# Attention projections: queries and keys computed for whole heads side by side and brought to their partitions by transfers

## The chip, the cores and the metric

The kernel runs on one core of one Trainium2 chip. The metric is the device time of one execution in microseconds (us); the time before is the median of three runs.

## What is computed

Four sequences of 512 tokens with 288 channels go through a transformer layer whose normalizations are shifted and scaled by a condition vector, and then through a rotation. Cut to what matters here:

```python
mod = silu(c) @ w_adaln + b_adaln                      # six vectors of 288 for each sequence
h = modulate(ln(x), sh_msa, sc_msa)
q, k, v = heads(h @ w_qkv + b_qkv)                     # 16 heads of 18 channels
o = softmax(q @ k.T * 18 ** -0.5) @ v
x = x + g_msa * (o @ w_proj + b_proj)
xn = modulate(ln(x), sh_mlp, sc_mlp)
x = x + g_mlp * top2_of_4_experts(xn)                  # hidden width 1152, gelu
U, _ = qr(P)                                           # P is 288 x 64
R = expm(skew(silu(c) @ W.T + b))                      # 64 x 64 for each sequence
x = x + ((x @ U) @ R - x @ U) @ U.T
```

## The kernel before, in words

Everything is float32, and the order of work on every engine is the order in which the program is written (`manual_schedule`): each engine and each DMA-issuing queue runs its own instructions in that order, and waits for others by semaphores.

**Attention.** A sequence (batch b, 0 to 3) is handled in four groups g of four heads, and a group in four key tiles t of 128 tokens: n = 4b + g, 64 steps (n, t) in all. A head has 18 channels but stands in a quarter of 32 partitions, so that a group fills the 128 partitions and four heads' small products run in the four quarters of TensorE at once. In each step `weigh` (line 1670) makes the scores z of four heads (line 1678, two tiles of two heads), ScalarE takes their exponentials es (line 1687), and `gather` (line 1691) adds the products with the values of the step before into av (line 1696). z has two buffers, so the scores of a step wait for the exponentials of the one before.

**Projections.** `project` (line 1645) makes a group's queries and keys: two products of three matmuls (line 1655), each 96 rows (a third of the 288 channels) by 128 columns (four heads of 32, 14 of each 32 columns being zeros in the padded weight `wqk`) by 512 tokens. ScalarE writes them to the tile `qk` and adds the bias (line 1662). So a batch takes eight such products. `begin` (line 1611) normalizes the next batch, turns it (`modulate_T`, line 1140, transposes into hT) and makes the values, with an add of the bias by VectorE (line 1632). The weights come zero-padded from the host.

**What else runs beside.** The lists `steps` and `beside` in the loop (lines 2172 to 2220) say, step by step, which pieces follow the scores: `steps[g, t]` holds those bound to a batch, `beside` gives one piece per step in order, after those of `steps`. They are:

- `divide` (`normalize`, line 1704): the softmax's sums. ScalarE copies av to oraw in the first step of the next group, SP moves the four rows of sums to den by four transfers (line 1718), VectorE inverts them two steps later (line 1724), SP moves them back to rr (line 1728), and VectorE spreads rr and multiplies in the step after (lines 1735 and 1736).
- `column` (line 1480): one reflection of the QR factorization, some 25 dependent VectorE instructions; the first such piece only scales pT.
- `merge`, `residual`, `route` (lines 1748, 1740, 1766): output projection po, the second normalization, the choice of experts. Its last pieces leave `where`, the slots of half of the tokens, and POOL then scatters rows to DRAM one by one (line 2008), which `load_slots` fetches again as xg.
- In `beside`: `other_modulation` (line 1189; products pr with `wadb`, then modrows, then POOL's DMAs through DRAM, lines 1213 and 1214), `skew_matrices` (line 1218; the load wr, the product pa in step 2.2 of batch 0, then 66 small stores udr by SP, line 1266, in eight pieces in the next eight steps, then the load um), and the matrix exponential (`rotations`, pieces pf, pw, ph, psq), which goes back and forth between TensorE and VectorE.

**The start.** SP loads the condition, the first part of the modulation's weights, the first batch, the first group's part of `wqk` (line 985), the rest of it (991), `wadb` (993), the biases badr (997), pT (1002), the other batches (1004) and small ones. VectorE clears the first values' tile vt (line 1045), POOL the second, and POOL's constants follow. `shift_scale`, the transposes, `project(0)` and the values precede the first step.

**After the attention** come the experts, in eight blocks, with TensorE busy throughout, the rest of the QR's columns beside them on VectorE, and at the end the rotation.

Of the kernel before, what the change touches and what calls it, by code (L numbers as in the profile page):

```python
# [10 lines left out]
F32 = mybir.dt.float32  # L11
# [7 lines left out]
P = 128  # L19
HD = 18  # L20
# [793 lines left out]
def fast_path(  # L814
# [139 lines left out]
    with ExitStack() as s1:  # L954
# [17 lines left out]
        bqk = const.tile([P, 2, NG], F32, name="bqk")  # L972
        nc.scalar.dma_start(out=bqk, in_=b_qk)
# [8 lines left out]
        wqk = wat.tile([CC, NK, 2, NG * P], F32, name="wqk")  # L982
        wqv = w_qk.rearrange("(k p) t f -> p k t f", p=CC)
        for i in range(2):
            nc.sync.dma_start(out=wqk[:, :, i, :P], in_=wqv[:, :, i, :P])
        wv = wat.tile([CC, NK, C], F32, name="wv")
        nc.scalar.dma_start(out=wv, in_=w_v.rearrange("(k p) f -> p k f", p=CC))
        bv = const.tile([P, C], F32, name="bv")
        nc.scalar.dma_start(out=bv, in_=b_v.partition_broadcast(P))
        for i in range(2):  # L990
            nc.sync.dma_start(out=wqk[:, :, i, P:], in_=wqv[:, :, i, P:])
        wadb = ada.tile([CC, NK, 4 * C], F32, name="wadb")
        nc.sync.dma_start(out=wadb, in_=wad[:, :, 2 * C :])
        badr = ada.tile([P, C], F32, name="badr")
        nc.gpsimd.memset(badr, 0.0)
        for i in range(4):
            nc.sync.dma_start(
                out=badr[i * HQ : i * HQ + B, :],
                in_=b_adaln[ds((2 + i) * C, C)].partition_broadcast(B),
            )  # L1000
        pt = rot.tile([D, C], F32, name="pt")
        nc.sync.dma_start(out=pt, in_=pT)
        for b in range(1, B):
            nc.sync.dma_start(
                out=xs[:, b * NT : (b + 1) * NT, :],
                in_=x[b].rearrange("(t p) c -> p t c", p=P),
            )
        bp = const.tile([P, C], F32, name="bp")
        nc.sync.dma_start(out=bp, in_=b_proj.partition_broadcast(P))
        wgT = const.tile([CC, NK, E], F32, name="wgT")  # L1010
        nc.sync.dma_start(out=wgT, in_=w_gate)
        b1s = const.tile([P, E, NF], F32, name="b1s")
        nc.sync.dma_start(out=b1s, in_=b1T)
        nc.sync.dma_start(out=wp, in_=w_proj.rearrange("g p c -> p g c"))
# [125 lines left out]
        def modulate_T(b, which, xh, k, dst):  # L1140
            pt = bank([P, N], f"pt{which}{b}{k}")
            for t in range(NT):
                nc.tensor.transpose(
                    pt[:CC, ts(t, P)], xh[:, t, ds(k * CC, CC)], ident
                )
            nc.scalar.activation(
                dst[:, k, :],
                pt[:CC, :],
                AF.Identity,
                bias=modT[:, 2 * which, k, b : b + 1],  # L1150
                scale=modT[:, 2 * which + 1, k, b : b + 1],
            )
# [36 lines left out]
        def other_modulation():  # L1189
# [5 lines left out]
            def product():  # L1195

                pr = bank([P, N], "pr")
                for k in range(NK):
                    for i in range(4):
                        nc.tensor.matmul(  # L1200
                            pr[ts(i, HQ), :C],
                            scp[:, k, :],
                            wadb[:, k, ts(i, C)],
                            start=(k == 0),
                            stop=(k == NK - 1),
                        )
                nc.vector.tensor_add(rows, pr[:, :C], badr)
                one = rows[2 * HQ : 3 * HQ, :]
                nc.vector.tensor_scalar_add(one, one, 1.0)
# [8 lines left out]
        def skew_matrices(between):  # L1218
# [10 lines left out]
            row = skew.tile([P, width], F32, name="row")  # L1229
# [379 lines left out]
        hTs, oTs, qks, avs, xhs = {}, {}, {}, {}, {}  # L1609
        
        def begin(b):
# [3 lines left out]
            hT = a2.tile([CC, NK, N], F32, tag="hT", name=f"hT{b}", bufs=1)  # L1615
# [6 lines left out]
            def values(t):  # L1622
                pv = bank([P, C], f"pv{b}{t}")
                for k in range(NK):
                    nc.tensor.matmul(
                        pv,
                        hT[:, k, ts(t, P)],
                        wv[:, k, :],
# [3 lines left out]
                nc.vector.tensor_tensor(  # L1632
                    vt[:, t, :, 0:HD],
                    pv.rearrange("p (h d) -> p h d", d=HD),
                    bv.rearrange("p (h d) -> p h d", d=HD),
                    ALU.add,
                )
# [7 lines left out]
        def project(n):  # L1645

            b, g = divmod(n, NG)
            qk = a2.tile([P, 2, N], F32, tag="qk", name=f"qk{n}")
            qks[n] = qk

            def product(i):
                hT = hTs[b]
                pq = bank([P, N], f"pq{n}{i}")
                for k in range(NK):
                    nc.tensor.matmul(  # L1655
                        pq,
                        wqk[:, k, i, ts(g, P)],
                        hT[:, k, :],
# [3 lines left out]
                nc.scalar.activation(  # L1662
                    qk[:, i, :], pq, AF.Identity, bias=bqk[:, i, g : g + 1]
                )

            return [lambda i=i: product(i) for i in range(2)]
# [3 lines left out]
        def weigh(n, t):  # L1670


            qk, es = qks[n], []
# [362 lines left out]
        for piece in turns + project(0) + values:  # L2036
            piece()
# [134 lines left out]
        for n in range(NN):  # L2172
# [24 lines left out]
            if n + 1 < NN:  # L2197
                query, key = project(n + 1)
                steps[g, int(g == 3)].insert(0, query)
                steps[g, 2].append(key)  # L2200
# [467 lines left out]
```

## Time and profile before

| what | us |
|---|---|
| median of three runs | 731.65 (731.27 to 734.58) |
| profiled execution | 733.85 |
| its span on the core | 732.1 |
| first scores z (the loop begins) | 26.7 |
| batch 0, 1, 2, 3 begin | 26.7, 98.9, 180.6, 263.9 |
| TensorE busy of the span | 704.6 (96%) |
| VectorE, ScalarE, POOL busy | 509.2, 278.5, 216.9 |
| the projections' matmuls (line 1655), 192 | 90.7 |
| exponentials (line 1687), 128 | 124.2 |

The span is the time on the core from the first to the last instruction, and the profiled execution's own time, 1.75 us more, is the number to set it against; the median of the runs is 2.2 us below that. A group's busy time is the union of its instructions, which overlap on TensorE. The timeline of an engine merges equal instructions that follow each other: start, length, engine, line, operation, output<-inputs, shapes, count, and in brackets the engine's idle time before and what ended it. SP's rows are its issues of transfers, not the transfers.

### The profile page before, as it was taken

To read this page: it belongs to the slowest core of one execution; us is meant where nothing else is said; L and a number is where in the kernel's file an instruction comes from. 1 tells how busy PE (TensorE), PEld (TensorE's weight loads), DVE (VectorE), ACT (ScalarE), POOL (GpSimd) and SP (SyncE) were. 2 spreads that over 40 slices of the span, in tenths; PEclk is the share of its full clock that TensorE was granted. 3 is DMA by queue.
4 is the path that set the end of the run, shared out by engine and by line. 5 is a ranking of instruction groups with operands and counts; after the bars stand their busy time and mean duration, and the time that the engine had idled before them with its cause. 6 is when DMAs were issued, how large, how long until landed. Compare 5 with 4: busy or idle time off the path is not lost. (4 is left out here: it accounts for less than half of the span.)

```text
span 732.1 us, 11398 instructions
## 1 busy us (share of the span) xinstructions
PE 704.6 (96%) x3627; PEld 404.2 (55%) x3627; DVE 509.2 (70%) x2237; ACT 278.5 (38%) x427; POOL 216.9 (30%) x311
## 2 busy tenths in 40 slices
PE   6999999999999999998999999999999999999995
PEld 5432334334353444324677776777667776676763
DVE  3565678796887879685268888888888886004335
ACT  2455554454525543474222423223233232221232
POOL 4035900620026013761047064441203123031110
PEclk9999999999999999999999999999999999999998
DMA  9547700000000001144252252365324153205044
GB/s 228 149 132 196 271 3 6 1 2 2 2 1 1 3 18 60 35 147 93 61 171 70 78 179 80 131 166 165 83 77 140 28 170 78 81 29 187 37 137 146
DMA packets 65511, 66.69 MB, mean 91 GB/s; under 512 B 31625, under 2 KB 55982, under 8 KB 65441
## 3 DMA queue, kind: packets, MB, share of 16 engines
q1 hardware_dynamic: 57376, 42.48, 21.0%
q0 software_dynamic: 7360, 22.91, 9.7%
q10 hardware_dynamic: 704, 0.49, 0.3%
q8 instruction: 30, 0.49, 0.3%
q14 instruction: 41, 0.33, 0.2%
HBM read 48.08 MB, written 18.09 MB: 90 GB/s over the span
## 5 line engine op out<-in xcount | busy, mean ns | idle before, releaser
L2356 PE MATMUL pe<-w2s,hm 128*128 128x288 f32 (+1 forms) x648 | 163.7, 408 | 0.0
L1687 ACT ACTIVATE es<-z 128x1024 f32<-128x1024 f32 x128 | 124.2, 1021 | 84.6 <-PE z L1678 84.0
L2296 PE MATMUL ph<-xgT,w1s 128*128 128x288 f32 (+2 forms) x576 | 151.8, 413 | 0.4
L2356 PEld LDWEIGHTS pe<-w2s,hm 128*128 128x128 f32 (+1 forms) x648 | 118.7, 187 | 31.5 <-issue 2.3
L2296 PEld LDWEIGHTS ph<-xgT,w1s 128*128 128x128 f32 x576 | 105.8, 190 | 40.2 <-issue 11.2
L2318 ACT ACTIVATE hm<-ph,b1r 128x576 f32<-128x576 f32 (+2 forms) x72 | 49.8, 737 | 131.1 <-PE ph L2309 121.2
L1678 PE MATMUL z<-qk 32*128 32x512 f32 x512 | 90.0, 640 | 3.0 <-ACT es L1687 2.8
L1655 PE MATMUL pq<-hT,wqk 96*128 96x512 f32 x192 | 90.7, 609 | 0.0
L1696 PE MATMUL av<-es,vt 128*32 128x512 f32 x512 | 69.1, 612 | 0.0
L1655 PEld LDWEIGHTS pq<-hT,wqk 96*128 96x128 f32 x192 | 34.3, 191 | 54.1 <-issue 39.4
L2371 POOL TENSOR_TENSOR y<-y,gb 128x288 f32<-128x288 f32 x32 | 27.3, 854 | 117.6 <-ACT y L2370 117.5
L2008 POOL DMA_INDIRECT slots<-xr,where x32 | 32.0, 1001 | 92.3 <-DVE where L2005 48.6
L2370 ACT ACTIVATE y<-pe,weight 128x288 f32<-128x288 f32 x32 | 16.0, 500 | 104.8 <-PE pe L2356 104.5
L2372 POOL DMA_INDIRECT chosen<-y,place x36 | 36.6, 1017 | 57.2 <-DVE y L2368 35.0
L1678 PEld LDWEIGHTS z<-qk 32*128 32x128 f32 x512 | 25.8, 182 | 48.4 <-ACT es L1687 30.7
L1762 POOL TENSOR_TENSOR xs<-xs,og 128x288 f32<-128x288 f32 x16 | 12.6, 801 | 125.8 <-DVE og L1761 125.8
L1478 DVE SCALAR_TENSOR_TENSOR q<-q 64x1 f32<-64x1 f32 (+1 forms) x192 | 44.2, 230 | 7.0
L1662 ACT ACTIVATE qk<-pq,bqk 128x512 f32<-128x512 f32 x32 | 22.0, 687 | 69.8 <-PE pq L1655 69.8
L1489 DVE STREAM_SHUFFLE wj<-pt 32x288 f32<-32x288 f32 (+47 forms) x96 | 42.1, 439 | 0.7
L1696 PEld LDWEIGHTS av<-es,vt 128*32 128x32 f32 x512 | 10.1, 108 | 48.1 <-issue 42.7
L1752 PE MATMUL po<-wp,oT 128*128 128x288 f32 x128 | 33.8, 412 | 1.2 <-DVE oT L1736 0.7
L1460 DVE SCALAR_TENSOR_TENSOR pt<-wj,uf,pt 64x288 f32<-64x288 f32 (+62 forms) x63 | 32.6, 517 | 2.2
(273 smaller groups left out, 901.5 us busy)
## 6 DMA issues: line engine op xcount, KB each, us to landing
w2s<-in_w_dram SPq DMA_DIRECT2D x8, 1296.0 KB
w1s<-in_w_dram SPq DMA_DIRECT2D x8, 1152.0 KB
slots<-empty POOLq DMA_DIRECT2D x36, 148.0 KB
yc<-chosen SPq DMA_DIRECT2D x4, 576.0 KB
out_dram<-xs SPq DMA_DIRECT2D x8, 288.0 KB
wr<-in_wrT_dram POOLq DMA_DIRECT2D x4, 567.0 KB
xg<-slots SPq DMA_DIRECT2D x4, 512.0 KB
xg<-slots SPq DMA_DIRECT2D x3, 640.0 KB
```

The lines of the kernel that those rows point to most:

```text
L1460: nc.vector.scalar_tensor_tensor(m, w, u[rows, :], m, ALU.mult, ALU.add)
L1478: nc.vector.scalar_tensor_tensor(s, u, part, s, ALU.mult, ALU.add)
L1489: nc.vector.stream_shuffle(wj[o : o + HQ, j:], pt[o0 : o0 + HQ, j:], [j % HQ] * HQ)
L1655: nc.tensor.matmul(pq, wqk[:, k, i, ts(g, P)], hT[:, k, :], start=(k == 0), stop=(k == NK - 1),)
L1678: nc.tensor.matmul(zs[c // 2][:, c % 2, :], qk[ts(c, HQ), 1, ts(t, P)], qk[ts(c, HQ), 0, :], start=True, stop=True,)
L1687: nc.scalar.activation(e, z, AF.Exp, scale=SCALE)
L1696: nc.tensor.matmul(avs[n][ts(c, HQ), :], vts[b % 2][:, t, 4 * g + c, :], es[c // 2][:, c % 2, :], start=(t == 0), stop=(t == NT - 1),)
L1752: nc.tensor.matmul(po, oTs[b][:, g, ts(t, P)], wp[:, g, :], start=(g == 0), stop=(g == NG - 1),)
L2296: nc.tensor.matmul(ph[:, j, :SB], w1s[:, k, ts(f, P)], xgT[:, k, ts(j, SB)], start=(k == 0), stop=False,)
L2318: nc.scalar.activation(hm[:, f, : CAPS[r]].rearrange("p (j s) -> p j s", j=NB), ph[:, :, :SB], AF.Gelu_apprx_tanh, bias=b1r[:, h, r, f : f ...
L2356: nc.tensor.matmul(po[ts(m, rows), :], slots_[:, f, :], w[:, f, :], start=(f == 0), stop=(f == NF - 1),)
L2372: nc.gpsimd.indirect_dma_start(out=chosen[h], out_offset=bass.IndirectOffsetOnAxis(ap=place[:, t : t + 1], axis=0), in_=y, in_offset=None, ...
```

## The change

Queries and keys are projected for seven heads at a time, without padding: five products a batch (items 0 to 4: queries of heads 0 to 6, keys of heads 0 to 6, the same of heads 7 to 13, and queries and keys of heads 14 and 15 together) of 126 or 72 columns. The result is copied to a tile `row`, and SP brings each head's 18 partitions to its quarter of a tile `qk0` to `qk3`, one per group, cleared once at the start by VectorE: 32 transfers a batch, 36 KB each. The biases become a 97th row of the first third of the weights, against a row of ones in hT that POOL writes. The weights are compacted on ScalarE from the padded ones, item by item; the padded tile `raw` later gives its place to `wadb`, and the loads from `wadb` on come after items 0 and 1 and their transfers. The values' result is copied by ScalarE. In the loop, items 2, 3 and 4 are made at steps 0.0, 0.2 and 1.0 of a batch (group.t), with their transfers at 0.1, 0.3 and 1.1; items 0 and 1 of the next batch at 3.0 and 3.1, their transfers at 3.1 and 3.2. The stored sum `row` of the skew matrices goes in place into `brs`.

```diff
+        HS = 7
+        wqk = wat.tile([CC + 1, NK, 5, HS * HD], F32, name="wqk")
+        raw = ada.tile([CC + 1, NK, 4 * C], F32, tag="raw", name="raw")
+        rawq = raw[:CC, :, : 2 * NG * P].rearrange("p k (t f) -> p k t f", t=2)
         wqv = w_qk.rearrange("(k p) t f -> p k t f", p=CC)
-        for i in range(2):
-            nc.sync.dma_start(out=wqk[:, :, i, :P], in_=wqv[:, :, i, :P])
...
+        for at, n in ((0, HS * HQ), (HS * HQ, (NH - HS) * HQ)):
+            for i in range(2):
+                nc.sync.dma_start(out=rawq[:, :, i, ds(at, n)], in_=wqv[:, :, i, ds(at, n)])
...
+        def parts_of(item):
+            if item < 4:
+                return [(0, item % 2, item // 2 * HS, HS)]
+            return [(0, 0, 2 * HS, 2), (2, 1, 2 * HS, 2)]
+
+        def in_groups(item):
+
+            out_ = []
+            for at, i, h, n in parts_of(item):
+                while n:
+                    m = min(n, 4 - h % 4)
+                    out_.append((at, i, h // 4, h % 4, m))
+                    at, h, n = at + m, h + m, n - m
+            return out_
+
+        def compact(item):
+            w = wqk[:CC, :, item, :].rearrange("p k (h d) -> p k h d", d=HD)
+            for at, i, h, n in parts_of(item):
+                nc.scalar.copy(
...
+            for at, i, g, c, n in in_groups(item):
+                nc.scalar.copy(w[:, ds(at, n), :], b[:, i, g, ds(c, n), :HD])
...
+        qks = []
+        for g in range(NG):
+            qk = wat.tile([P, 2, N], F32, name=f"qk{g}")
+            nc.vector.memset(qk, 0.0)
+            qks.append(qk)
...
+        def late_loads():
+            for i in range(4):
+                nc.sync.dma_start(
+                    out=badr[i * HQ : i * HQ + B, :],
+                    in_=b_adaln[ds((2 + i) * C, C)].partition_broadcast(B),
+                )
+            nc.sync.dma_start(out=pt, in_=pT)
...
-            row = skew.tile([P, width], F32, name="row")
+            row = brs
...
+            hT = a2.tile([CC + 1, NK, N], F32, tag="hT", name=f"hT{b}", bufs=1)
+            nc.gpsimd.memset(hT[CC : CC + 1, 0, :], 1.0)
...
-                nc.vector.tensor_tensor(
-                    vt[:, t, :, 0:HD],
-                    pv.rearrange("p (h d) -> p h d", d=HD),
-                    bv.rearrange("p (h d) -> p h d", d=HD),
-                    ALU.add,
-                )
+                nc.scalar.copy(vt[:, t, :, 0:HD], pv.rearrange("p (h d) -> p h d", d=HD))
...
+        def project(b, item):
+
+            n = HD * sum(m for *_, m in parts_of(item))
+            row = a2.tile([HS * HD, N], F32, tag="row", name=f"row{b}{item}")
+
+            def product():
                 hT = hTs[b]
-                pq = bank([P, N], f"pq{n}{i}")
+                pq = bank([P, N], f"pq{b}{item}")
                 for k in range(NK):
+                    rows = CC + (k == 0)
                     nc.tensor.matmul(
-                        pq,
-                        wqk[:, k, i, ts(g, P)],
-                        hT[:, k, :],
+                        pq[:n],
+                        wqk[:rows, k, item, :n],
+                        hT[:rows, k, :],
...
-                nc.scalar.activation(
-                    qk[:, i, :], pq, AF.Identity, bias=bqk[:, i, g : g + 1]
-                )
...
+                nc.scalar.copy(row[:n], pq[:n])
+
+            def spread():
+                for at, i, g, c, m in in_groups(item):
+                    for h in range(m):
+                        nc.sync.dma_start(
+                            out=qks[g][ds((c + h) * HQ, HD), i, :],
+                            in_=row[ds((at + h) * HD, HD), :],
+                        )
...
-        for piece in turns + project(0) + values:
+        compact(0)
+        compact(1)
+        for piece in turns:
+            piece()
+        for item in range(2):
+            for piece in project(0, item):
+                piece()
+        for item in range(2, 5):
+            compact(item)
+        wadb = ada.tile([CC + 1, NK, 4 * C], F32, tag="raw", name="wadb")
+        nc.sync.dma_start(out=wadb[:CC], in_=wad[:, :, 2 * C :])
+        late_loads()
+        for piece in values:
             piece()
...
-            if n + 1 < NN:
-                query, key = project(n + 1)
-                steps[g, int(g == 3)].insert(0, query)
-                steps[g, 2].append(key)
+            if g == 0:
+                for item, (made, spread) in zip(
+                    (2, 3, 4), (((0, 0), (0, 1)), ((0, 2), (0, 3)), ((1, 0), (1, 1)))
+                ):
+                    pieces = project(b, item)
+                    steps[made].insert(0, pieces[0])
+                    also(spread, pieces[1])
+            if g == 3 and b + 1 < B:
+                pieces = [*project(b + 1, 0), *project(b + 1, 1)]
+                for step, piece in zip(((3, 0), (3, 1), (3, 1), (3, 2)), pieces[:1] + pieces[2:3] + pieces[1:2] + pieces[3:]):
+                    also(step, piece)
```

Before, the first group's part of the padded weights was loaded alone; now four loads bring the padded weights to `raw`, seven heads first. `b_qk` and `b_v` come as one row each on ScalarE's queue.

## The prediction

> A step is named group.t: "1.0 of batch 1" is group 1, t = 0. All times are of the profiled execution (span 732.1 us, time 733.85), 2.2 above the median of the runs, 731.65; differences worked out on it are added to the median at the end.
>
> **What bounds the kernel now.** I read the page's busy line and slices first.
>
> ```profile
> PE 704.6 (96%) x3627; PEld 404.2 (55%) x3627; DVE 509.2 (70%) x2237; ACT 278.5 (38%) x427; POOL 216.9 (30%) x311
> ...
> PE   6999999999999999998999999999999999999995
> ```
>
> TensorE is busy from the second slice on: at first sight a saved product is a saved time. The busy times by stage (start, the four batches, the experts; after the length come PE, PEld, DVE, ACT, POOL) say more:
>
> ```profile
> 26.70:98.90 72.20, 70.78 (x387) 24.23 (x386) 48.56 (x217) 40.00 (x46) 36.72 (x64) 1.00 0.51 158
> 98.90:180.60 81.70, 77.74 (x403) 30.70 (x402) 64.96 (x278) 40.57 (x48) 16.08 (x21) 1.00 0.02 3
> 180.60:263.90 83.30, 81.48 (x455) 34.23 (x454) 67.81 (x279) 40.47 (x48) 16.16 (x21) 1.00 0.01 2
> 263.90:344.40 80.50, 77.76 (x423) 31.16 (x423) 62.83 (x273) 40.99 (x52) 37.65 (x42) 0.98 0.23 66
> ```
>
> In batches 1 and 2 VectorE is 65 to 68 us busy out of 82 to 83; its chains of small instructions add some 5 us of gaps under 0.15 us. TensorE's waits in batch 1 are for VectorE's chain or POOL's share of it: 0.9 at pf (POOL xr), 0.8 at pw, 0.8 at pt. In batch 3 one wait counts:
>
> ```profile
> PE pt L2090 <- DMA xg<-slots: 1.9, 1, 1.9
> ```
>
> TensorE reaches the first transposes of the gathered rows 1.9 us before they land. They hang on POOL's 16 scatters, one per 2.77 us, begun at 267.56 once VectorE had "where" at 267.1: batch 3 is set by that row of scatters, not by TensorE.
>
> **What a product is worth.** The timeline of TensorE in batch 3:
>
> ```profile
> 316.28 2.84 PE L1655 MATMUL pq<-hT,wqk 96*128 96x512 f32 x6
> 319.05 1.14 PE L1678 MATMUL z<-qk 32*128 32x512 f32 x8
> 320.12 1.06 PE L1696 MATMUL av<-es,vt 128*32 128x512 f32 x8
> 321.36 2.04 PE L1678 MATMUL z<-qk 32*128 32x512 f32 x8 [0.18 <-ACT es L1687]
> 323.33 1.07 PE L1696 MATMUL av<-es,vt 128*32 128x512 f32 x8
> 324.33 1.39 PE L1678 MATMUL z<-qk 32*128 32x512 f32 x8
> ```
>
> A step with a product and the empty one after it take 5.74 + 2.31 = 8.05. Two empty steps take 2.97 + 2.31 = 5.28, since the scores then wait for exponentials. A product less is 2.77 on TensorE. There are 20 instead of 32: 3 fewer in each batch (1.2, 2.0, 2.2 and 3.2 lose one, 3.0 gains one), 8.3 a batch, 33 in all if nothing else binds. A 97-row, 126-column product is priced like the 96*128 rows: z on 32 rows (0.64 each) and av on 32 columns (0.61) take no less, so neither gain nor loss is seen from shape.
>
> **The start.** Four memsets of 1024 columns go ahead of vt's on VectorE: 4 x 0.88 (half of L1045's 1.76) = 3.5. VectorE itself was idle until 6.72, which hides them. But POOL's first vt column waits for vt, and its run of 5.6 (3.13 to 8.71) then ends at 12.2; the two rs instructions (1.38) end at 13.6 instead of 10.55. Normalizing (1.45) and nine more transposes at 0.23 put the first product at 17.2 instead of 15.27. ACT's two compactions, 2 x (0.47 + 2 x 0.21) by the 96x384 and 96x12 rows, lie before hT's activations; uncovered they cost at most 1.8. Products end at 22.7; values 5.9 more, their banks now freed by ACT behind three compactions (3.4): first scores at 28.8 instead of 26.7, **+2.1**.
>
> The spreads: no row shows 18 partitions of 2 KB. Issue rows on SP run from 0.25 (badr) and 0.36 (udr) to 0.63 (den, also SBUF to SBUF, gap included). I take 0.55, near den, and 1.7 to landing (den issued at 44.91, first packets at 46.20). Spread 0 from 20.7, spread 1 to 28.4; the first scores need the first four of spread 1, 28.5: just hidden by the values.
>
> Behind them on SP stand wadb and all late loads. Wadb also waits for ACT's last compaction (26.7), which the spreads hide. It is issued at 28.4 rather than 7.1; with 6 to 7 us of transfer (11.99 to 18.76 before) it lands at 35.7, pT at 36.2, against 27 at need. VectorE's order is first (1.2), column 0 (5.75), then modrows: 43.2 instead of 34.2. Who waits for modrows?
>
> ```profile
> 34.95 0.81 POOL L1213 DMA_DIRECT2D mdr<-modrows  x1 [24.14 <-DVE modrows L1207]
> ...
> 51.30 0.55 POOL L1214 DMA_DIRECT2D gates<-mdr  x1 [3.70 <-DMA mdr<-modrows]
> 52.13 2.76 POOL L1233 DMA_DIRECT2D wr<-in_wrT_dram  x4 [0.28 <-issue]
> ```
>
> POOL's four round trips, then wr, whose packets end at 65.9: 31.7 after modrows, so 74.9 now. TensorE wants wr in 2.2 (pa): 71.33 before; now, with the saved products, at 32.6 + 19.0 (0.1 to 1.1) + 10.6 (four empty steps) + 3.1 = 65.3. It waits 9.6. The 8.3 of batch 0 are gone and pa starts **3.6 later** than before.
>
> **SP at the border of batches 0 and 1.**
>
> ```profile
> 100.02 4.93 SPq L1266 DMA_DIRECT2D udr<-row  x13
> 105.06 2.45 SPq L1718 DMA_DIRECT2D den<-oraw  x4
> 107.55 8.39 SPq L1266 DMA_DIRECT2D udr<-row  x23
> 116.04 2.44 SPq L1728 DMA_DIRECT2D rr<-den  x4
> 118.52 5.55 SPq L1266 DMA_DIRECT2D udr<-row  x16
> ```
>
> SP is already full here with the skew stores. Scores at 1.0 of batch 1 now need head 7, whose key comes with the first transfer of spread 3, written behind the stores of 0.2. From spread 0 (13.3 before batch 1 begins, at T) SP must issue 22 spreads (12.1), 57 stores (20.8 at 0.365) and three quartets den/rr (7.5): T + 27.1, landed T + 28.8. Before, 1.0 began at T + 15.2. TensorE waits 13.6; then 1.0 and 1.1 run in 15.5 (16.8 before): **+12.3** at 1.2. VectorE has run out of columns by then, so this wait is nobody's gain.
>
> What comes back: the other 8.3 of batch 1 run into VectorE, whose idle in that stretch is 2.7 and which loses four value adds (1.8): **-4**. In batch 2, spread 3 stands behind rr, issued 194.43 to 196.9; plus 0.55 and 1.7 is 199.1 against 196.44: **+2.7**. Afterwards VectorE loses adds and their waits for pv (1.66, 1.58, 1.00): **-5.5** until "where". Batch 3: the scatters begin 9.1 later, TensorE's 8.3 become a wait at xg; POOL's merges, held by a spread wait like batch 2's, add **+1**. What remains, 10.1, passes to the experts, where TensorE is 97% busy. Sum: 3.6 + 12.3 - 4 + 2.7 - 5.5 + 1 = +10.1; 731.65 + 10.1 = **742**.
>
> Moved: ACT's value copies (0.47) replace VectorE's adds, and ACT in 3.0 has 5.1 + 1.2 in 7.8. The hT row memset (0.1 to 0.5 by POOL's rows) stands behind rs; nobody waits. If late q1 loads hold spreads 2 and 3 in batch 0, 1.0 there slips to about 50, inside the 9.6.
>
> [...] The four den issues in 2.45 show that SP's issues overlap their landings, so I stay with the rows.
>
> **Rivals.** (1) Faster: SP's queue does not bind, because spreads and stores issue in less than the rows say or 1.0 finds head 7 landed. It decides below 28.5 us of SP work between spread 0 and head 7 (I count 40.4; with 0.25 per spread still 33.8). Then the 12.3 is gone and batch 0 ends about 2 early: -2 - 4 - 5.5 = -11.5, **720** (713 to 728). For it: TensorE's 96%; against: the SP rows above. Chance 0.2. (2) About the same: a spread costs 0.25 (-6.6 at the border, -1.8 at the start) and batches 1 and 2 give 4 more: **730** (728 to 735), 0.15. (3) My forecast, 735 to 750, 0.5. (4) Worse: 0.63 per spread (+3.1) and landings late as rr's beside wr (issued from 51.8, packets until 60.8), or spread 1 behind an rr that VectorE delays, 3 at two batch borders: **751** (750 to 762), 0.12. (5) The products' 33 come through, less the start's 2.1: **700**, 0.03; batch 3's scatters and VectorE speak against it. Should the change save no TensorE time at all, that is within (4): most of it is forecast to be lost anyway.
>
> **Numbers.** 0.5% of 731.65 is 3.7, about what this measurement tells from no change: 728.0 to 735.3. Faster 0.2 + 0.03 = 0.23, same 0.15, slower 0.5 + 0.12 = 0.62. The range 720 to 757 leaves out half of (1), (5) and half of (4): 0.19. The prices 0.25 to 0.63 alone span 733 to 745.
>
> **What would show it.** L1655's successor with 120 matmuls instead of 192; modrows near 43; TensorE waiting for wr at pa; SP's first spread of item 3 in batch 1 behind the stores, with scores waiting some 13 us; scatters beginning near 276; a wait of some 10 for xg. I am wrong if scores at 1.0 don't wait for a spread, if pT lands before 30, or if batches 1 and 2 each shrink by 8.

## The result and the profile after

The changed kernel takes 771.59 us (770.70 to 773.59), the kernel before 731.46 beside it: a ratio of 1.0543 (1.0506 to 1.0581). The profiled execution took 771.0, its span is 769.3, 37.2 longer than before. The forecast was 742 in a range of 720 to 757: the sign was right, the size was not, and the time lies outside the range.

The page of the changed kernel, busy time and slices:

```profile
PE 704.3 (92%) x3555; PEld 400.0 (52%) x3555; DVE 506.9 (66%) x2225; ACT 279.9 (36%) x449; POOL 217.8 (28%) x315
...
PE   5998899495999789997799999999999999999995
...
PEclk9999796696999989999799999999999999999998
```

The projections' line has 120 matmuls with 63.5 us instead of 192 with 90.7, yet TensorE is as long busy as before (704.6): the scores z take 104.6 instead of 90.0 and av 73.6 instead of 69.1. Some of these instructions ran at half the clock, which the row PEclk shows as 6 and 7, and some scores ran one head after the other (see the border of batches 0 and 1). By stage (the start, batches 0 to 3, the experts; columns as before):

```profile
0.00:30.30 30.30, 21.08 (x84) 15.20 (x84) 9.47 (x19) 11.07 (x28) 8.56 (x55) 1.00 0.42 102
30.30:113.70 83.40, 75.32 (x367) 24.02 (x366) 46.95 (x217) 40.79 (x49) 36.78 (x65) 0.92 0.67 194
113.70:218.40 104.70, 85.75 (x384) 31.54 (x384) 64.89 (x286) 39.79 (x49) 16.66 (x22) 0.79 0.07 15
218.40:301.70 83.30, 75.42 (x440) 32.27 (x440) 64.88 (x266) 39.72 (x49) 16.62 (x22) 0.94 0.07 16
301.70:383.10 81.40, 71.38 (x405) 28.88 (x405) 61.58 (x266) 38.81 (x50) 37.39 (x42) 0.92 0.26 74
383.10:769.30 386.20, 375.39 (x1883) 268.06 (x1881) 259.16 (x1174) 109.77 (x226) 101.83 (x109) 0.99 0.38 111
```

Batch 2 is as long as before (83.3) with 6 us less TensorE work in it: the saved products became idle time there. Batch 1 is 23 longer. Set against the forecast, step by step (the times at which a step's scores begin, after less before):

| stretch | forecast | measured |
|---|---|---|
| up to the first scores | +2.1 | +3.65 |
| from there to the end of pa (2.2 of batch 0) | +1.5 | +10.96 |
| from there to batch 1 | 0 | +0.2 |
| batch 1 up to 1.2 | +12.3 | +21.6 |
| from 1.2 to batch 2 | -4 | +1.3 |
| batches 2 and 3 | +2.7 - 5.5 + 1 | +1.0 |
| experts and rotation | 0 | -1.5 |
| sum | +10.1 | +37.2 |

**The start and pa.** SP's issues in the changed kernel:

```profile
22.62 10.76 SPq L1709 DMA_DIRECT2D qk<-row  x14
33.48 0.41 SPq L2094 DMA_DIRECT2D wadb<-in_w_adaln_dram  x1
33.99 1.34 SPq L1045 DMA_DIRECT2D badr<-in_b_adaln_dram  x4
35.38 0.58 SPq L1049 DMA_DIRECT2D pt<-in_pT_dram  x1
```

Fourteen transfers of heads take SP 10.76, or 0.77 each; the forecast took 0.55. Everything behind them is late by that much. VectorE stands still for pT:

```profile
42.59 0.45 DVE L1489 TENSOR_REDUCE size<-pt 64x1 f32<-64x288 f32 x1 [26.27 <-DMA pt<-in_pT_dram]
```

and POOL, which must have modrows, comes to wr at 69.2 instead of 52.13:

```profile
50.25 0.81 POOL L1257 DMA_DIRECT2D mdr<-modrows  x1 [34.85 <-DVE modrows L1251]
...
69.20 2.76 POOL L1277 DMA_DIRECT2D wr<-in_wrT_dram  x4 [0.43 <-ACT oraw L1763]
```

**The border of batches 0 and 1.** SP again:

```profile
100.34 6.43 SPq L1709 DMA_DIRECT2D qk<-row  x7
106.87 1.91 SPq L1310 DMA_DIRECT2D udr<-brs  x5
108.88 2.47 SPq L1776 DMA_DIRECT2D rr<-den  x4
111.45 5.29 SPq L1709 DMA_DIRECT2D qk<-row  x7
116.79 4.53 SPq L1310 DMA_DIRECT2D udr<-brs  x13
121.42 2.46 SPq L1766 DMA_DIRECT2D den<-oraw  x4
123.92 2.50 SPq L1310 DMA_DIRECT2D udr<-brs  x7
126.52 5.70 SPq L1709 DMA_DIRECT2D qk<-row  x7
132.32 5.48 SPq L1310 DMA_DIRECT2D udr<-brs  x16
137.89 2.46 SPq L1776 DMA_DIRECT2D rr<-den  x4
140.40 5.84 SPq L1310 DMA_DIRECT2D udr<-brs  x16
146.35 5.30 SPq L1709 DMA_DIRECT2D qk<-row  x7
```

SP never rests here. The last row is the spread with head 7's key, and TensorE's scores of 1.0 stop for it after three of their four heads (two instructions each):

```profile
136.54 2.04 PE L1726 MATMUL z<-qk 32*128 32x512 f32 x6 [0.17 <-ACT es L1735]
148.52 2.07 PE L1726 MATMUL z<-qk 32*128 32x512 f32 x2 [9.94 <-DMA qk<-row]
150.52 1.94 PE L1744 MATMUL av<-es,vt 128*32 128x512 f32 x8
152.38 4.96 PE L1697 MATMUL pq<-hT,wqk 97*72 97x512 f32 x6
157.17 4.05 PE L1800 MATMUL po<-wp,oT 128*128 128x288 f32 x16
```

av then takes 1.94 instead of 1.06: the clock is at half from 139.7 for 17.1 us.

Not every wait for a head shows as one. The spread of item 1, the row at 111.45, reaches into batch 1, whose first scores begin at 113.69:

```profile
113.69 4.33 PE L1726 MATMUL z<-qk 32*128 32x512 f32 x8 [0.31 <-DMA qk<-row]
```

The four heads start at 113.69, 114.45, 115.23 and 115.95, one per transfer, instead of together, and the eight instructions take 4.33 instead of 1.14. The profile counts this as busy.

**Where the products went.** The waits of TensorE in the changed kernel (columns: total, times, longest):

```profile
PE z L1726 <- DMA qk<-row: 10.2, 2, 9.9
PE pt L2150 <- DMA xg<-slots: 9.5, 2, 4.9
PE psq L1441 <- DVE XY L1436: 6.7, 1, 6.7
...
PE pf L1379 <- DVE sqa L1367: 6.4, 1, 6.4
```

Before, they were 1.9 at xg and 0.9 at pf (for POOL xr), and the other two were not there. The wait at pf lies in batch 1 and that at psq in batch 2: there the saved products ended. Before, pf came 14.2 after the scores of 1.2, with two products between:

```profile
130.85 1.14 PE L1678 MATMUL z<-qk 32*128 32x512 f32 x8
...
132.92 2.84 PE L1655 MATMUL pq<-hT,wqk 96*128 96x512 f32 x6
...
141.31 2.84 PE L1655 MATMUL pq<-hT,wqk 96*128 96x512 f32 x6
145.07 0.25 PE L1335 MATMUL pf<-fs,every 64*64 64x4 f32 x2 [0.92 <-POOL xr L1777]
```

After, it comes 14.2 after them without any:

```profile
167.29 1.14 PE L1726 MATMUL z<-qk 32*128 32x512 f32 x8
...
174.01 1.07 PE L1744 MATMUL av<-es,vt 128*32 128x512 f32 x8
181.45 0.37 PE L1379 MATMUL pf<-fs,every 64*64 64x4 f32 x2 [6.37 <-DVE sqa L1367]
```

From the scores of 1.2 to pf VectorE works through its row (the second normalization, a division, the rotation's first instructions) and is 12.45 of 14.2 us busy, after as before. That stretch is 14.1 to 14.2 in every run below that has the same order there and no idle matmuls, except for 15.0 in e2, whatever TensorE does beside it.

### The profile page after: what moved, and what is told of

It reads as the page before. It is cut to its first block, busy times and chain, and to the rows that moved or that the text cites. A ratio compares the mean times of both kernels' runs of the same rounds, so it can differ in the third digit from the quotient of the medians.

```text
span 769.3 us, 11559 instructions
## 1 busy us (share of the span) xinstructions
PE 704.3 (92%) x3555; PEld 400.0 (52%) x3555; DVE 506.9 (66%) x2225; ACT 279.9 (36%) x449; POOL 217.8 (28%) x315
## 5 line engine op out<-in xcount | busy, mean ns | idle before, releaser
L1726 PE MATMUL z<-qk 32*128 32x512 f32 x512 | 104.6, 690 | 11.8 <-DMA qk<-row 10.2
L1744 PE MATMUL av<-es,vt 128*32 128x512 f32 x512 | 73.6, 649 | 0.0
L1726 PEld LDWEIGHTS z<-qk 32*128 32x128 f32 x512 | 31.8, 196 | 63.6 <-ACT es L1735 33.5
L1697 PE MATMUL pq<-hT,wqk 96*126 96x512 f32 (+3 forms) x120 | 63.5, 671 | 0.0
L1697 PEld LDWEIGHTS pq<-hT,wqk 96*126 96x126 f32 (+3 forms) x120 | 22.6, 200 | 39.1 <-issue 35.3
L1809 DVE TENSOR_TENSOR og<-po,gates 128x288 f32<-128x288 f32 x16 | 7.3, 455 | 44.2 <-PE po L1800 44.1
```

Of the source, the lines that this page charges most:

```text
L1697: nc.tensor.matmul(pq[:n], wqk[:rows, k, item, :n], hT[:rows, k, :], start=(k == 0), stop=(k == NK - 1),)
L1726: nc.tensor.matmul(zs[c // 2][:, c % 2, :], qk[ts(c, HQ), 1, ts(t, P)], qk[ts(c, HQ), 0, :], start=True, stop=True,)
L1744: nc.tensor.matmul(avs[n][ts(c, HQ), :], vts[b % 2][:, t, 4 * g + c, :], es[c // 2][:, c % 2, :], start=(t == 0), stop=(t == NT - 1),)
```

## The experiments

All ratios are against the kernel before, run on the same chip.

**Theory.** The loss is the place of 128 transfers at 0.77 in SP's row (loads behind them at the start, themselves behind the stores at the border), and it is not paid back since a saved product is worth nothing where other engines set the end. **Rivals:** the saved products are worth their time and are lost elsewhere; the halved clock is the loss; a late start alone carries it.

**e1: late loads early.** Compactions 2 to 4, wadb, badr and pT before the transposes.

```diff
         compact(1)
+        for item in range(2, 5):
+            compact(item)
+        wadb = ada.tile([CC + 1, NK, 4 * C], F32, tag="raw", name="wadb")
+        nc.sync.dma_start(out=wadb[:CC], in_=wad[:, :, 2 * C :])
+        early_loads()
         for piece in turns:
```

> The changed kernel, with all five compactions, wadb, badr and pT ahead of the transposes and of the first two spreads. Theory (queue order at the start): modrows, at 49.4 in the changed kernel, comes at about 41, wr and pa some 8 earlier, the start itself 1 later because the compactions delay hT; 771.6 becomes about 763 (760 to 767). Rival (the clock or the products themselves cost the time): within 2 of 771.6.

Measured 771.25 (1.052, 1.0481 to 1.0559): nothing. VectorE has pT at 27.2 instead of 42.6, but modrows comes only 1.7 earlier (47.7, where I expected 41): it now waits for the product pr, which comes only at 45.9, behind scores that wait for heads. The step of pa ends at 85.8 instead of 88.6, and the wait for heads at 1.0 of batch 1 grows to 12.5. SP's row at the border takes the little that was won.

**e2: the 66 stores by POOL.**

```diff
-                        nc.sync.dma_start(
+                        nc.gpsimd.dma_start(
                             out=udr[r, :, ds(r + 1 + lo - at, hi - lo)],
```

> The changed kernel, with the 66 skew stores issued by POOL and not by SP. Theory (SP's queue at the border of batches 0 and 1): spread 3 of batch 1 lands before step 1.0, whose wait of 9.9 goes, with the half clock after it; 757 (752 to 763), a few us of it given back where POOL's merges stand behind the stores. Rival (late loads at the start are all of it): 768 or more.

Measured 753.11 (1.0273, 1.0243 to 1.0303), 18.5 less. The waits of the scores for heads, 10.2 in all, are gone. The stores now stand in front of POOL's own work:

```profile
119.74 22.42 POOL L1310 DMA_DIRECT2D udr<-brs  x44
142.17 1.55 POOL L1810 TENSOR_TENSOR xs<-xs,og 128x288 f32<-128x288 f32 x2
```

**e3: e1 and e2 together** (no new edit).

> Early loads and stores by POOL together. Theory: the two costs are separate places and add, 749 (742 to 756), still slower than the 731.5 of before, as VectorE and the scatters keep the saved products. Rival (the two are one wait passed on): not under 757.

Measured 755.08 (1.0251, 1.0169 to 1.0333; single runs 746.3 to 759.1): not to be told from e2. The step of pa ends at 81.3, 7.3 earlier than in the changed kernel, but the scores at the start of batch 1 wait 4.25 for the spread written behind rr in 3.2, and 1.2 comes at 146.22, where e2 has 145.58. A gain of 4 by the early loads is not seen in the profiled execution; the spread of the single runs does not rule it out.

**e4: no transfers at all.**

```diff
             def spread():
-                for at, i, g, c, m in in_groups(item):
...
+                pass
```

> The changed kernel without its 128 transfers: the tiles of queries and keys stay zero, so the softmax is uniform; products, copies and compactions remain. It shows what the transfers cost and what the 36 matmul groups less are worth. Theory: 733 (725 to 742): no wait at 1.0 of batch 1, wadb 5 earlier, but the saved products go into VectorE's chain and the scatters. Rival (the transfers are the whole difference and the products are worth their 33): about 705.

Measured 742.16 (1.0119, 1.0082 to 1.0155): by the ratios 31 of the 40 us are the transfers' doing, and 9 remain although TensorE has fewer products (56.3 us busy with them instead of 90.7). The scores are all zero in this kernel, so its output is not the layer's.

**e5: the kernel before, with a third of the products' depth left out.**

```diff
-                for k in range(NK):
+                for k in range(NK - 1):
...
-                        stop=(k == NK - 1),
+                        stop=(k == NK - 2),
```

> The kernel before, with the last third of the 288 channels left out of every query and key product: 64 matmuls of 192 are gone, two of six in each group, by the rows 0.92 us of TensorE per pair half, 2.77/3 x 32 = 29.5 us less on TensorE, and no other work added or moved. That is nearly what the change takes away (33), without its transfers, its memsets or its later loads. Theory A (a saved product is worth its time only in batch 0 and up to 1.2 of batch 1; afterwards VectorE's chain, the rotation's pieces and the row of scatters set the end): batch 0 gives up to 7 until it meets wr (pa), batch 1 up to 3, the rest nothing: 731.65 - 8 = 723, 718 to 728. Rival B (products are worth their time everywhere, and the changed kernel loses it again elsewhere): 731.65 - 29.5 = 702, 698 to 710.

Measured 726.37 (0.9894, 0.9846 to 0.9943). Some 28 us of TensorE work less (0.86 in each of 32 steps by the timeline) are worth 6 to 8: 5.8 by the medians, 7.8 by the ratio, 7.0 at the end of the loop. At the end of pa all 5.2 of batch 0 are there; at the start of batch 1 0.45 is left, since the values then wait 3.5 for their bank behind VectorE:

```profile
PE po L1752 <- DVE oT L1736: 4.2, 3, 2.6
PE pt L2090 <- DMA xg<-slots: 3.7, 1, 3.7
PE pv L1625 <- DVE vt L1632: 3.5, 1, 3.5
```

This separates the theory from the rival that products are worth their time.

**e6: idle matmuls in TensorE's waits** (on e2), so that the clock stays up.

```diff
+        def warm(to, count):
+            for _ in range(count):
+                nc.tensor.matmul(to, ident[:, : to.shape[0]], every, start=True, stop=True)
...
+                warm(pa[:, :P], 24)
...
+                warm(pf[:, :P], 32)
```

> The changed kernel with half of e2's edit kept (all 66 stores by POOL, so no wait of the scores at 1.0 of batch 1), and idle matmuls in front of four waits of TensorE, so that it does not stand still there: 24 of 128 columns before pa, 32 before pf, 28 before the first psq, 48 before the first transposes of xg (a matmul of 128 columns some 0.21 us at the full clock: 5, 7, 6 and 10 us). They write a tile that the real product then overwrites. e2 had 753.1 with some 54 us of the loop at half the clock. Theory A (the halved clock after a wait costs TensorE real time, since it is busy in the steps that follow): the half clock goes from most of these places and the time falls by 6 to 12, to 745 (741 to 748). Rival B (the halved clock is only a sign of the waits; what follows is set by other engines anyway): 753, within 2, or a little more where the idle matmuls run past the end of a wait.

Measured 751.66 (1.0251, 1.0204 to 1.0298) beside e2's 1.0273: the same within their intervals, while the mean clock rose from 0.961 to 0.988. The 24, 32, 28 and 48 idle matmuls took 5.62, 7.41, 6.33 and 10.98, some 0.23 each where I expected 0.21. The first scores of batch 1 come 3.3 earlier than in e2, but by pf that is more than gone (163.3, in e2 160.6): VectorE waits 6.4 for POOL, which is at the stores until 143.6. The steps around psq and xg are 2.3 and 2.4 shorter. So the halved clock is worth 2 to 3 at a place, and little of it reaches the end: it does not explain e2's 20. The two longest stretches at half clock in the first half of the changed kernel, at 115.8 and 139.7 in batch 1, are absent from e2 together with the waits, so their price was not measured apart. Rival B was nearer; Theory A's 6 to 12 fell.

By the clock records of its trace the changed kernel's loop has eight stretches at a granted clock of 0.5, of 3.41, 10.24, 13.65 or 17.07 us, 82 us in all. At 1.0 of batch 1 the clock falls 1.1 us after the last matmul (138.58 to 139.69) and stays at half for 8.2 us of matmuls after the wait (148.52 to 156.76), and it falls at 115.8 while scores of single heads are running. Had TensorE worked through all 82 us at the pace of the rows of av and pq there (1.94 instead of 1.06, 4.96 instead of 2.80), an estimated 36 to 37 us would be lost to the clock. e6 took the loop's half-clock time from 54.6 us in e2 to 13.7 and won 1.4, within the intervals; TensorE still waits 3.4 at pf for VectorE there.

**e7: four places mended.** Tiles cleared behind the values' tile, badr and pT loaded at their old place, wadb by POOL, item 1's transfers ahead of rr in 3.2, every second store by POOL.

```diff
+        for qk in qks:
+            nc.vector.memset(qk, 0.0)
+
         rrows = []
...
-        nc.sync.dma_start(out=wadb[:CC], in_=wad[:, :, 2 * C :])
+        nc.gpsimd.dma_start(out=wadb[:CC], in_=wad[:, :, 2 * C :])
...
+                    if step == (3, 2):
+                        steps[step].insert(0, piece)
```

> The changed kernel with its order mended at four places, the same work otherwise: the queries' and keys' tiles are cleared on VectorE after the values' tile instead of before; badr and pT are loaded at their old place, and wadb by POOL, so that none of them stands behind the first 14 transfers of heads; the seven transfers of the key of heads 0 to 6 go ahead of the inverses' in 3.2; every second skew store is issued by POOL. Theory A (these four places carry what the change loses up to batch 1, and the border of batches 0 and 1 no longer passes it on): first scores near 28, modrows near 37, pa done by 77, batch 1 begins by 103, and no wait for a head at 1.0: 743 (738 to 748). Rival B (as with the early loads alone, what is won at the start is met by the next wait): as with the stores alone, 753 (750 to 756).

Measured 773.88 (1.0542, 1.0493 to 1.0591): nothing. The first scores start at 26.77, as before the change, and stop after one head for 3.6 and again for 0.6: they want the first eleven of the fourteen transfers. Wadb, which POOL now issues at 24.95, shares their time; whether it holds them up was not tried. The scores of 1.0 of batch 1 wait 9.1: 34 of the stores still stand in SP's row there, and head 7's key is issued at 135.5, behind them. Modrows comes at 47.7 and the step of pa ends at 86.1, so the start is not mended either. Both of my numbers for this run fell.

**e8: e7 with e6's idle matmuls** (no new edit).

> The order of e7 and the idle matmuls of e6 together. Theory A (order and clock are two losses that add up): what e7 gives less 5 to 10, at 736 (731 to 742). Rival B (the clock is only a sign of the waits): the same as e7 within 2.

Measured 768.55 (1.0479, 1.0437 to 1.0521), 5 below e7, at the bottom of what Theory A gave for the difference, but with e7's level missed it settles little.

**e9: heads 0 to 3 first at the start, all stores by POOL** (on e7).

```diff
+        for piece, spread in made:
+            piece()
+            spread(0, 4)
+        for piece, spread in made:
+            spread(4)
```

> The changed kernel with all its work, and the order mended as in e7, but with the two things that e7 got wrong put right: at the start the transfers of heads 0 to 3 of both items go first (eight, 6.2 us at 0.77) and the other six behind them, so that the first scores need not wait for fourteen; and all 66 skew stores are issued by POOL. Theory A (the loss up to batch 1 is where each transfer stands in SP's row): first scores near 28, modrows near 38, no wait for a head at 1.0 or 3.3: batch 1 begins near 104 and 1.2 of it comes near 136, 10 earlier than with the stores by POOL alone: 743 (739 to 747). Rival B (some other wait takes what the start gives, as it did for the early loads): 753 (750 to 756).

Measured 765.68 (1.0465, 1.0432 to 1.0498; single runs 758.5 to 769.2). The trace is of the fastest of them. The start is mended: first scores at 27.1 and pa done at 74.86, 0.85 later than before the change. It does not last. In 3.0 TensorE waits 3.6 for a bank behind VectorE's columns, and item 3's transfers stand behind rr, which waits for VectorE (SP in e9):

```profile
110.17 5.66 SPq L1711 DMA_DIRECT2D qk<-row  x7
119.77 2.65 SPq L1778 DMA_DIRECT2D rr<-den  x4
122.51 5.28 SPq L1711 DMA_DIRECT2D qk<-row  x7
```

SP is idle from 115.8 to 119.8 with head 7 next in its row. The scores of 1.0 wait for it, 3.6 in batch 1 and 3.3 in batch 2. Both of my numbers, 743 and 753, were too low.

**e14: item 3 made at 0.1, its transfers ahead of rr** (on e9).

```diff
-                    (2, 3, 4), (((0, 0), (0, 1)), ((0, 2), (0, 3)), ((1, 0), (1, 1)))
+                    (2, 3, 4), (((0, 0), (0, 1)), ((0, 1), (0, 2)), ((1, 0), (1, 1)))
...
-                    also(spread, pieces[1])
+                    steps[spread].insert(0, pieces[1])
```

> e9 with items 3 and 4 handled so that their transfers go ahead of the inverses' on SP: item 3 is made at 0.1 and its transfers are the first thing in 0.2, item 2's the first in 0.1, item 4's the first in 1.1. In e9 the seven transfers with head 7's key stood behind rr, and rr behind VectorE's columns (SP waited until 119.8 and began them at 122.5; the scores of 1.0 wanted them at 121.2). Theory A (the waits of e9 at 1.0 of batches 1 and 2, 3.6 and 3.3, and the halved clock in the 10 us after them, go): 10 to 14 below e9's 765.7 and 758.5 at its best, 752 (746 to 757). Rival B (the inverses, now behind the transfers, bring the divisions late and po waits for them instead): 760 to 770.

Measured 753.75 (1.0276, 1.0246 to 1.0306), 12 below e9: the waits at 1.0 of batches 1 and 2 are gone, as Theory A said. Part of Rival B came too: 1.0 of batch 0 now waits 4.1 for a head, po 5.6 for divisions that are late, and xg takes 12.8. It is no better than e2.

**e10 and e11: the piece of `beside` first in each step**, on e9 and on the kernel before.

```diff
+                if beside:
+                    beside.pop(0)()
                 for piece in steps[g, t]:
                     piece()
-                if beside:
-                    beside.pop(0)()
```

> e9 with one more edit: in every step the piece of the list beside goes ahead of those bound to the batch, so that VectorE takes the rotation's small instructions before the second normalization and the routing. Theory A (in 2.0 to 2.2 of batches 1 and 2 TensorE waits some 6 us at pf and at psq only since VectorE has other work in front of what they need, and the saved products lie in that wait): both waits go, 6 to 8 us less than e9, 736 (732 to 741). Rival B (VectorE's whole work between 1.1 and 2.2 is what takes the time, in whatever order): the same as e9 within 3.

> The kernel before with the same edit alone as e10 adds to e9. TensorE of the kernel before waits under 1 us at any of these places (pf 0.9, pw 0.8, psq none), so there is little to win: theory A 730 (727 to 733). Rival B (other pieces are now late, as modrows would have been early and the divisions behind them): slower, 735 to 742.

Measured 777.01 (1.0591, 1.0562 to 1.062) and 758.89 (1.0365, 1.0339 to 1.0392): slower both times, by 11 and 26. In e11 po waits 6.6 and 3.2 behind the rotation's instructions and 2.8 for a division, where it waited 1.2 in all: VectorE's order is tight in the kernel before, and Theory A of e11 fell.

e10 says less. The waits at pf and psq do go, as its Theory A had it (pf comes 7.7 after the scores of 1.2, not 14.2). But pw then waits 7.3, and from 1.2 to batch 2 it is only 2.1 shorter than e9. The edit also moves the load um ahead of item 3's transfers on SP, where it comes after POOL's stores, which are issued until 136.5 (SP in e10):

```profile
137.74 0.50 SPq L1317 DMA_DIRECT2D um<-udr  x1
138.34 5.28 SPq L1711 DMA_DIRECT2D qk<-row  x7
```

The scores of 1.0 of batch 1 wait 17.1 for that last row, 13.5 more than in e9: the loss of e10 is again SP's row, and its 777 does not judge VectorE's order.

**e12: e4 with e7's order.**

> e4 (no transfers of heads at all: the queries and keys in the groups' tiles stay zero, so the scores are zero) with e7's order: tiles cleared behind the values' tile, badr and pT at their old place, wadb by POOL. It asks what the 8.7 us are by which e4 is slower than the kernel before, although it has 33 us of products less and no transfers. Theory A (the delayed start: hT 3 late behind the memsets, pT 9 late, and through modrows and wr pa): first scores near 26.5, modrows near 37, 734 (730 to 737). Rival B (they come later, from 2.0 of batch 1 on, where the kernel without products waits for VectorE and POOL in any case): 741 (739 to 744).

Measured 739.13 (1.0077, 1.0052 to 1.0103). At the low end of Rival B's range, above Theory A's: 3 less than e4, with intervals that overlap. pa ends at 73.1, 0.9 earlier than before the change, and from there the kernel loses what it had: the wait for a bank behind VectorE in 3.0 (3.2), pf 6.4, psq 6.6, xg 9.9. A kernel without transfers, with its loads in place and with a third less time in products on TensorE, is still slower than the one before.

**e13, e15, e16: the values' bias and ScalarE's copies alone**, on the kernel before. The row of ones is written by POOL in 2.3, by VectorE there, and by ScalarE:

```diff
-        wv = wat.tile([CC, NK, C], F32, name="wv")
+        wv = wat.tile([CC + 1, NK, C], F32, name="wv")
...
+            if k == 0:
+                nc.gpsimd.memset(dst[CC : CC + 1, 0, :], 1.0)
...
-                nc.vector.tensor_tensor(
+                nc.scalar.copy(vt[:, t, :, 0:HD], pv.rearrange("p (h d) -> p h d", d=HD))
```

> The kernel before with one part of the change alone: the values' bias as a 97th row of their weights and of hT, and the values copied by ScalarE (0.47 us each) instead of added by VectorE. Queries and keys stay as before. Theory A (from 1.2 of batch 1 on the end of each stage is set by VectorE's chain, so that 16 adds of 0.46 us off VectorE, and its waits of 18.9 us for pv, are worth time where saved products are not): 728 (724 to 731). Rival B (these adds stood in VectorE's slack, and ScalarE's copies now stand in front of exponentials in 3.0 to 3.3): the same or slower, 731 to 737.

Measured 748.03 (1.0196, 1.0168 to 1.0225). One row of 512 ones cost it:

```profile
PE pv L1629 <- POOL hT L1144: 12.2, 1, 12.2
```

POOL was at the slots' clears (11.14 us from 76.27) in front of it. From 3.1 of batch 0 on no step is more than 1.3 longer, and those of the VectorE chain are 0.3 to 1.0 shorter, 2 in all.

> e13 with the row of ones written by VectorE instead of POOL, where it stood behind 33 clears of the slots in 2.3 of batch 0 and held the values' product for 12.2 us. Apart from that one place every step of e13 had the length it has in the kernel before, within 0.1, except 1.0 of batch 1 (1.0 shorter), 1.0 and 1.1 of batch 2 (0.8 shorter) and the start (0.3 later). Theory A (VectorE's relief is worth only that): 731 (729 to 733). Rival B (the relief is worth 3 or more once the hold is gone): 728 or less. If a copy by ScalarE costs exponentials, over 734.

Measured 748.13 (1.0223, 1.02 to 1.0247): the same trap on another engine. In 2.3 of batch 0 VectorE is still at its columns, and its row of ones comes at 89.24; TensorE waits 9.9. A second wait of 1.8 of the same kind makes 11.7 in all. None of the three explanations that I gave named this.

> e13 and e15 with the row of ones copied by ScalarE just ahead of the activation that fills the same tile, so that it stands behind nothing that is late: the values' bias in the weights and the copies by ScalarE, and nothing else of the change. Theory A (VectorE's relief is worth what the steps of e13 and e15 away from the hold show, 0.4 at 3.3 of batch 0, 1.0 at 1.0 of batch 1 and 0.8 in batch 2, less 4 copies of some 0.5 on ScalarE): 730 (728 to 732). Rival B (worth 5 or more): 727 or less. Rival C (the copies hold exponentials): over 733.

Measured 736.35 (1.0055, 1.0036 to 1.0075): with nothing late in front of the row the part alone wins nothing and costs 4, as Rival C had it. Steps 3.0 and 3.1 of batch 2 are 1.5 and 2.5 longer; TensorE's waits for ScalarE's hT at the values rise from 1.2 to 3.3. VectorE's relief of the adds (509.2 to 504.7 us busy) is worth at most the 2.2 us by which four steps of e13, e15 and e16 alike are shorter (3.3 of batch 0, 1.0 of batch 1, 1.0 and 1.1 of batch 2).

No kernel here that does the whole work is faster than the one before; the best of the changed ones (e2, e3, e6, e14) are 2.5 to 2.8% slower.

## Why the prediction was right and wrong

**Right:** the sign, and the places. The start's chain over pT, modrows and wr, the wait at pa, the row of SP at the border with head 7 last, a wait of about 10 at 1.0 of batch 1 (9.94; forecast 13.6 after an earlier arrival) and one of 9.5 at xg are where they were put. The counts of the border hold: 57 stores took 20.3 (forecast 20.8) and three quartets 7.4 (7.5).

**Wrong, step by step:**

1. *"I take 0.55, near den."* A transfer of heads costs SP 0.77 (its 18 packets of 2 KB take some 118 ns each and all begin within 0.3 us by the packet records, while the issue holds SP for 0.71: it is the issue that costs, not the bytes). This is a mis-sized term, and outside the bounds given (0.25 to 0.63). At the border 22 of them took 18.2 instead of 12.1, so head 7 landed at 34.8 after batch 1's start, not 28.8: 6.0 of that stretch's missing 9.3.
2. *"Then 1.0 and 1.1 run in 15.5."* They ran in 18.8 after the wait, with the clock at half for the first 8.2: the other 3.3. The rows of head 7's scores (2.07), av (1.94) and pq (4.96) take 4.0 more than the same rows at the full clock (1.12 in e7, 1.06, 2.80). The forecast had no term for the clock.
3. *"Wadb is issued at 28.4, it lands at 35.7, pT at 36.2."* Issued at 33.5 (a transfer price of 3.1 and a start 1.9 later), VectorE had pT at 42.6; modrows 49.4 instead of 43.2; POOL's row from mdr to wr took 18.95 instead of 17.2; and pa's matmuls stretched over wr's pieces at half the clock until 88.6, where 77.6 was forecast. With the start's 1.5 these are 11 us. The mechanism was right, each size too small, and all errors lay on one chain, so they added up. That mending the start alone brings little is shown by e9, not by e1, where modrows came only 1.7 earlier: e9's step of pa ends at 74.86, all stores are off SP, and it still takes 765.68, as the next waits are in VectorE's and SP's rows.
4. *"-4"* in batch 1 and *"-5.5"* by the relief of VectorE: neither came (+1.3 and about 0). This step failed in mechanism. I had counted VectorE's busy time and the adds taken off it as if the stage were bound by the sum of its work. Up to pf it is bound by the row of instructions on VectorE that starts with po's result (14.2 from the scores of 1.2 to pf, before and after), and the adds do not stand in it. e5 (28 us of products worth 6 to 8) and e16 (the adds worth 2 at most) show both halves. Which row binds the rest of batches 1 and 2 was not worked out; e10, which takes the wait at pf away, finds the next one at pw.
5. *"+2.7"* in batch 2 did not come: head 7's key was issued at 232.96, and the scores of 1.0, begun at 234.22, need it only for their last head; I had asked for it at the step's start.

Rival (1), faster if SP does not bind, took SP out of the way as its condition; e2 did just that, and stayed at 753, not 720: points 3 and 4 are still in it.

**What stays open:** the 5 to 6 us by which e12 is still slower than the kernel before are spread over pf, psq, xg and a bank in 3.0; which of ScalarE's copies, the new order of the products or VectorE's backlog starts them was not separated.

## What to carry to other kernels

A saved instruction was worth its time here only where its engine ended last (28 us of products were worth 6 to 8 in e5): leave part of it out in a copy of the old kernel (as e5 does) and see what that is worth before paying for the saving with transfers. Price every added transfer on its issuing queue by a measured row of the same shape (0.55 was taken here from other shapes, 0.77 was measured), multiply by all that stand between it and its reader, and look for what waits in front of it: an instruction put into the row of a late engine is late itself, however small (one row of ones held TensorE for 12.2 us in e13 and 9.9 in e15). Where several late terms lie on one chain, their errors add (11 us up to the end of pa here), and the range must allow for all of them at once.

## What the runs showed of the hardware

- The issue of a transfer from 18 partitions to 18 others, 2 KB each, held SP's queue for 0.71 us and came every 0.77; a row to 32 partitions (den) came every 0.62, a small store of four partitions 0.36 on SP and 0.51 on POOL's queue.
- TensorE's granted clock went to 0.5 in the changed kernel's loop in or just after waits of 1.2 to 9.9 us, and twice (33.9 and 115.8) while or just after scores of single heads ran one after the other; the stretches last 3.41, 10.24, 13.65 or 17.07 us, and that at 1.0 of batch 1 outlasts the wait by 8.2. With idle matmuls of 128 columns in four waits (some 0.23 us each; 48, which the trace shows as 96 instructions, in 10.98) 13.7 us of e6's loop were at half, where e2 had 54.6.
- Four heads' scores that are released by one transfer each, 0.77 apart, run one after the other: 4.33 us instead of 1.14, all of it counted as busy (the clock is at 0.5 from 115.8 on, in the last head's scores).
- Memsets of four 4 KB tiles ahead of another on VectorE cost 4.3 us there (0.91 each, one per 1.07; the other tile's memset begins at 5.60, in e7, where it goes first, at 1.30), and by POOL's wait for that tile the first transposes come 2.65 later (15.27, in e7 12.62).
